# A selective-scan kernel: D·u added by the third scan, loads for the chained sums issued sooner, memsets issued later

## The chip, the cores and the metric

The kernel runs on one core of a Trainium2 chip. The metric is the device time of one execution in microseconds, as the median of several executions. All timed executions quoted below are in the fast state; one experiment was executed only once, and its state is unknown, which is said there. The ratios compare kernels that ran on the same chip in the same rounds.

Five engines matter: TensorE (PE, with its weight loads PEld), VectorE (DVE), ScalarE (ACT), GpSimd (POOL), and SyncE (SP), which here only issues transfers, all of them from one queue in program order.

## The reference

The reference is one vision block on a 4x64x64x96 image: group norm, a convolutional branch with a four-direction selective scan, then linear attention and a small quantized feed-forward network. The change touches the scan and what follows it.

```python
def selective_scan(u, delta, A, Bs, Cs, D, delta_bias):     # K = 4 directions, Dn = 192, N = 16, L = 4096
    delta = jax.nn.softplus(delta + delta_bias[None, :, :, None])
    def step(h, inp):
        ut, dt, Bt, Ct = inp
        dA = jnp.exp(dt[..., None] * A[None])
        h = dA * h + (dt * ut)[..., None] * Bt[:, :, None, :]
        y = jnp.einsum('bkdn,bkn->bkd', h, Ct)
        return (h, y)
    ...
    return y + D[None, :, :, None] * u
...
# the four directions: rows, columns, and both of them backwards
inv_y = jnp.flip(out_y[:, 2:4], axis=-1)
y = out_y[:, 0] + inv_y[:, 0] + wh_y + invwh_y
# layer norm of y, times silu(z), projection; x = x + that
# t = tokens of x
t = t + attention(norm(t))          # q (k^T v), six heads
t = t + ffn(norm(t))
```

D·u can be added in any one direction, with the four D summed, since u is the same array in another order. That is the freedom that the change uses.

## The kernel before

The scan is cut into 1536 pieces: 4 batches, 4 directions in the order `KORD` = 1, 3, 0, 2, 4 chunks of 1024 time steps, 6 groups `g` of 32 channels, and 4 quarters `q` of the state. A piece is a 128x1024 tile. I call the 96 pieces of one batch and direction a stage. One piece takes:

- (First, per group of four pieces, SyncE loads two tiles named dl: delta, and delta·u.)
- ACT: `dA = exp(anm·dl)` into PSUM, two buffers, emitted one piece ahead.
- GpSimd: `w = dl·B`, emitted four pieces ahead ("inject").
- DVE: the scan `h = dA·h + w`, in one instruction.
- The product `w = h·C`: on DVE (903 pieces) or on GpSimd (633), dealt by a tally of estimated costs.
- PE: sums the product over the state into `yp` in PSUM (one buffer), three pieces late. In the last quarter of a group it also adds what earlier directions left, which `load_sums` has fetched into the tile `ya`. These are the chained sums.
- ACT: copies `yp` to SBUF every eight pieces ("ys"), and SyncE stores it two pieces later.

```python
p = SimpleNamespace(w=pool("wp", 9), ..., ya=pool("yap", 1), ..., dl=pool("dlp", 3), ...)

def load_sums(self, i):
    b, e, ci, g, q = self.pieces[i]
    k = KORD[e]
    if k < 2:
        return
    at = CH * (NCH - 1 - ci)
    t = c.p.ya.tile([128, 3, 256], F32, name=f"ya_{i}", tag="ya")
    whole = lambda d: d.rearrange("h p l -> (h p) l")
    srcs = [c.yd[1][b]] if k == 3 else [c.yd[0][b], whole(c.y13[b]), whole(c.ud[b])]
    for j, src in enumerate(srcs):
        c.nc.sync.dma_start(t[:, j], src[32 * g : 32 * g + 32, at : at + CH].rearrange("d (x l) -> x d l", x=4))
    self.sums[i // NQ] = [(t[:, j, ::-1], c.dskip[:, g] if j == 2 else c.back4) for j in range(len(srcs))]

def reduce(self, i):
    ...                                   # y: the PSUM tile, prod: the product w
    more = self.sums.pop(i // NQ, []) if q == NQ - 1 else []
    for x in range(4):
        c.nc.tensor.matmul(y[32 * x : 32 * x + 32, g % 2, :], c.sum4, prod[:, 256 * x : 256 * x + 256], ...)
    for n, (src, w) in enumerate(more):
        c.nc.tensor.matmul(y[:, g % 2, :], w, src, start=False, stop=(n == len(more) - 1))

# the scan's loop, one turn per piece
for i in range(n):
    self.loads(i)                 # at q == 3: dl of the group three ahead, 2 x 512 KB; B and C now and then
    if i % NQ == NQ - 1:
        ...                       # (waits in program order until the turned y is made)
        self.load_sums(i)
    if i >= 1:
        self.carry(i - 1)         # ACT
    if i % 8 == 3 and i > 8:
        self.evacuate(i - 4)      # ACT: ys
    if i + 1 < n:
        self.decay(i + 1)         # ACT: dA
    if i >= 3:
        self.reduce(i - 3)        # PE
    if i + AHEAD < n:
        self.inject(i + AHEAD)    # GpSimd
    self.late_product()           # GpSimd
    self.scan(i)                  # DVE
    c.later.tick()                # SyncE: stores that are due
    ...                           # one step each of: the next deltas, the other work ("back")
```

Beside the scans, one step per piece, run the next batches' prologue and the epilogue of the batch that is done. Two pieces of it are touched besides the memsets:

```python
c.vec.tensor_tensor(m0, self.vks, c.hmask, ALU.mult)      # middle(): 96x96, once per batch

while nxt:                                                # last(): attention and its residual, per 512 tokens
    q, tt = nxt
    x1 = ln.load("x1b", f"x1b{q}", [96, 512])
    nc.sync.dma_start(x1, c.x1d[b][:, cols])
    ...
    c.vec.tensor_tensor(x2, ps, x1, ALU.add)
```

Of the kernel before, what the change touches and what calls it, by code (L numbers as in the profile page):

```python
# [11 lines left out]
F32 = mybir.dt.float32  # L12
# [4 lines left out]
ALU = mybir.AluOpType  # L17
# [4 lines left out]
NB, IH, IW, DM = 4, 64, 64, 96  # L22
# [3 lines left out]
CH = 1024  # L26
NCH = L // CH
HID = 384
NQ8 = L // 512
NG, NQ = DN // 32, NS // 4  # L30
# [23 lines left out]
def hybrid_kernel(ctx: ExitStack, tc: tile.TileContext, a: dict, out: bass.AP):  # L54
    nc = tc.nc
# [3 lines left out]
    def pool(name, bufs, **kw):  # L59
        return ctx.enter_context(tc.tile_pool(name=name, bufs=bufs, **kw))  # L60

    const, dram = pool("const", 1), pool("dram", 1, space=DRAM)
    p = SimpleNamespace(
        w=pool("wp", 9), y=pool("yp", 2), cy=pool("cyp", 2), h=pool("hp", 2), ya=pool("yap", 1), pu=pool("pup", 1), pd=pool("pdp", 2),
        f=pool("fp", 8), bc=pool("bcp", 5), dl=pool("dlp", 3), dA=pool("dAp", 2, space=PSUM),
        ps=pool("psp", 1, space=PSUM),
    )
# [33 lines left out]
    c = SimpleNamespace(nc=nc, a=a)  # L101
# [55 lines left out]
    def weights():  # L157
# [200 lines left out]
        dg = temp("dg", [128, 3, 2])  # L358
        nc.vector.tensor_copy(dg, ps[:, 0:6].rearrange("p (g h) -> p g h", h=2))
        for g in range(NG):  # L360
            nc.vector.tensor_scalar(dskip[:, g], back4, dg[:, g % 3, g // 3 : g // 3 + 1], None, ALU.mult)
        nc.vector.memset(on192, 1.0 / DN)
        nc.vector.memset(on96, 1.0 / DM)
        nc.vector.tensor_scalar(mean96, i96, -1.0 / DM, None, ALU.add)
# [112 lines left out]
def prologue(c, b, xts=None):  # L477
# [11 lines left out]
    with tc.tile_pool(name=f"xg_{b}", bufs=1) as xgp:  # L489

        xg = xgp.tile([128, 2, L], F8, name=f"xg_{b}", tag="xg")
        xgw = xg.bitcast(F32)
        nc.gpsimd.memset(xgw[64:128, 1], 0.0)
        with tc.tile_pool(name=f"cv_{b}", bufs=1) as cvp:
            xsT = cvp.tile([DM, L], F8, name=f"xsT_{b}", tag="xsT")
            tflat = [cvp.tile([96, (IH + 2) * (IW + 2)], F8, name=f"tp{h}_{b}", tag=f"tp{h}") for h in range(2)]
# [40 lines left out]


            sub.close()
            for h in range(2):  # L540
                nc.gpsimd.memset(tflat[h].bitcast(F32), 0.0)
            for h in range(2):
# [96 lines left out]
        with tc.tile_pool(name=f"rw_{b}", bufs=1) as rw:  # L639
# [4 lines left out]
            tbg, sgg = (t.rearrange("p (g r) -> p g r", r=64) for t in (tbc, sgn))  # L644
            g2 = rw.tile([128, 2, 320], F8, name=f"g_{b}", tag="g")
            gw = g2.bitcast(F32)
            nc.gpsimd.memset(gw[:, :, 48:80], 0.0)
            for o in (1, 0):
                xr = rw.tile([128, 96, 64], BF16, name=f"xr{o}_{b}", tag="xr")
                xm = xr.rearrange("p (m i) g -> p i m g", m=3)  # L650
# [27 lines left out]
                for gh in range(2):  # L678
# [41 lines left out]
                        )  # L720
                    yield
                c.later.flush()
                for x, k in enumerate((o, o + 2)):
                    nc.sync.dma_start(gw[:, x, 0:48], c.sgd[b][k].rearrange("(p f) -> p f", p=128))
                    yield
                    yield
                    gp = bank(f"gp{k}", k // 2).rearrange("p (s f) -> p s f", s=4)
                    for s in range(4):
                        nc.tensor.matmul(
                            gp[:, s, :], g2[:, x, 48 * s : 48 * s + 128], c.ident8, start=True, stop=True  # L730
                        )
                    yield
                    t = rw.tile([48, 4, 32], F32, name=f"gt_{b}_{k}", tag="gt", bufs=2)
                    nc.scalar.activation(t.bitcast(F8), gp[0:48], AF.Copy, saturate=False)
                    nc.sync.dma_start(c.gTd[b][k], t)
# [30 lines left out]
class Epilogue:  # L766
# [9 lines left out]
    def open(self):  # L776
        c, p, b = self.c, self.c.p, self.b
        ep = self.ep = self.ctx.enter_context(c.tc.tile_pool(name=f"ep_{b}", bufs=1))
        self.vks = ep.tile([DM, DM], F32, name=f"vks_{b}", tag="vks")
        self.ms = [ep.tile([DM + (i == 2), DM], F32, name=f"m{i}_{b}", tag=f"m{i}") for i in range(3)]  # L780

        tts = [ep.tile([DM + 1, 512], F32, name=f"tt{i}_{b}", tag=f"tt{i}") for i in range(2)]
        for tt in tts:
            c.nc.gpsimd.memset(tt[DM : DM + 1, :], 1.0)
        self.lane = SimpleNamespace(
            f32=lambda nm: p.f.tile([128, 512], F32, name=f"{nm}_{b}", tag="f"),
            bank=lambda nm, j: p.ps.tile([128, 512], F32, name=f"{nm}_{b}", tag=f"b{j}"),
            load=lambda key, nm, shape, dt=F32: ep.tile(shape, dt, name=f"{nm}_{b}", tag=key),
            tts=tts, x={},
        )  # L790
        self.opened = True
# [63 lines left out]
        return r  # L855

    def sums(self, ln):
        nxt = None
        while nxt is not None or self.todo or not self.opened:
            q, nxt = nxt, None  # L860
            if q is None:
                q = self.take()
                if q is None:
                    yield
                    continue
                self.loads(ln, q, ("ys", "sz", "xb"))
                yield
                yield
            got = []
            yield from self.norm(ln, q, got)  # L870
            nxt = got[0]
# [117 lines left out]
    def middle(self):  # L989
        c, nc, ln, mm = self.c, self.c.nc, self.lane, self.mm  # L990
        c.later.flush()
        m0, m1, m2 = self.ms
        c.vec.tensor_tensor(m0, self.vks, c.hmask, ALU.mult)
        ps = ln.bank("m1", 1)[0:96, 0:96]
        mm(ps, [(m0, c.wff)])
        yield
        nc.scalar.copy(m1, ps)
        ps = ln.bank("m2", 0)[0 : DM + 1, 0:96]
        mm(ps, [(c.wqT, m1)])
        yield  # L1000
        c.vec.tensor_tensor(m2, ps, c.bff, ALU.add)

    def last(self, ln):
# [3 lines left out]
        def fetch(n):  # L1007
# [4 lines left out]
            nc.sync.dma_start(tt[0:96, :], c.td[b][:, 512 * q : 512 * q + 512])  # L1012
            return q, tt

        def bank(nm, j):
            return ln.bank(f"{nm}{q}", j)

        n = 0
        nxt = fetch(n)
        while nxt:  # L1020
            q, tt = nxt
            cols = slice(512 * q, 512 * q + 512)
            x1 = ln.load("x1b", f"x1b{q}", [96, 512])
            nc.sync.dma_start(x1, c.x1d[b][:, cols])
            n += 1
            nxt = fetch(n)

# [6 lines left out]
            yield  # L1034
            x2 = f32("x2")[0:96]
            c.vec.tensor_tensor(x2, ps, x1, ALU.add)
            pc = bank("fc", 1)[0:96]
            mm(pc, [(c.mean96, x2)])
            yield
# [49 lines left out]
class Scans:  # L1089
# [173 lines left out]
    def load_sums(self, i):  # L1263

        c = self.c
        b, e, ci, g, q = self.pieces[i]
        k = KORD[e]
        if k < 2:
            return
        at = CH * (NCH - 1 - ci)  # L1270
        t = c.p.ya.tile([128, 3, 256], F32, name=f"ya_{i}", tag="ya")
        whole = lambda d: d.rearrange("h p l -> (h p) l")
        srcs = [c.yd[1][b]] if k == 3 else [c.yd[0][b], whole(c.y13[b]), whole(c.ud[b])]
        for j, src in enumerate(srcs):
            c.nc.sync.dma_start(  # L1275
                t[:, j], src[32 * g : 32 * g + 32, at : at + CH].rearrange("d (x l) -> x d l", x=4)
            )
        self.sums[i // NQ] = [(t[:, j, ::-1], c.dskip[:, g] if j == 2 else c.back4) for j in range(len(srcs))]

    def reduce(self, i):  # L1280

# [28 lines left out]
    def run(self, back):  # L1310
        c, lanes, n = self.c, [], len(self.pieces)

        w = [c.p.w.tile([128, CH], F32, name=f"w_s{x}", tag="w") for x in range(7)]
        ps = [c.p.dA.tile([128, CH], F32, name=f"dA_s{x}", tag="dA") for x in range(2)]
        for x in range(3):
            half = slice(512 * (x % 2), 512 * (x % 2) + 512)
            lanes.append(
                self.prepare((
                    w[x].rearrange("p (t l) -> p t l", t=2), w[3 + x // 2][:, half], w[5 + x // 2], ps[x // 2][:, half],
                ))  # L1320
            )
        interleave(lanes)
        for q in range(NQ):
            self.load_bc(0, self.bt, 0, 0, 0, q)
            self.load_bc(1, self.ct, 0, 0, 0, q)
        while lanes:
            interleave(lanes)
            c.later.tick()
        c.later.flush()
        self.load_dl(0)  # L1330
        for m in (1, 2):
            self.load_dl(m)
        self.decay(0)
        for i in range(AHEAD):
            self.inject(i)
        for i in range(n):
            self.at = i
            self.loads(i)
            if i % NQ == NQ - 1:
                while KORD[self.pieces[i][1]] == 2 and self.pieces[i][0] not in c.turned:  # L1340
                    next(back)
                self.load_sums(i)
            if i >= 1:
                self.carry(i - 1)
            if i % 8 == 3 and i > 8:
                self.evacuate(i - 4)
            if i + 1 < n:
                self.decay(i + 1)
            if i >= 3:
                self.reduce(i - 3)  # L1350
            if i + AHEAD < n:
                self.inject(i + AHEAD)
            self.late_product()
            self.scan(i)
            c.later.tick()
            if i % 8 == 1 and self.todo:
                while (self.todo[0][0], self.todo[0][1] % 2) not in c.ready:
                    next(back)
                lanes.append(self.prepare())
            interleave(lanes)  # L1360
            next(back, None)
            if i > n - 64:
                next(back, None)
        self.late_product()
        for i in range(n - 3, n):
            self.reduce(i)
        self.evacuate(n - 1)
        c.later.flush()
        self.at = 2 * n
# [76 lines left out]
```

## Time and profile before

| | before |
|---|---|
| median of 3 runs | 5713.55 us (5709.6 to 5714.53) |
| span of the profiled run | 5710.5 us, mean granted TensorE clock 0.663 |
| DVE / POOL busy | 5157.6 / 5075.9 us |
| ACT / PE busy | 3566.1 / 3355.5 us |
| DVE idle by direction 1, 3, 0, 2 (over four batches) | 70, 46, 49, 138 us |

DVE and POOL are the full engines; the idle in the stages is what a change of waits can win. The last row comes from cutting the trace at every 96th decay and taking the length of each stretch less DVE's busy time; it is one profiled run and good to about 5 us a cell.

The prediction shows the page, the stretches and one hole. Here are lines that it only quotes or does not have, from the list of waits: who waited, for whom, then the total in us, how many times, and the longest.

```profile
POOL w L401 <- DVE h L401: 121.5, 106, 4.2
...
DVE x L401 <- DMA x1b<-x1d: 13.4, 4, 4.6
```

GpSimd waits 106 times for DVE's `h`, while DVE waits for a product of GpSimd in 31 us in all; and one load, `x1b`, stops DVE itself. The next list is that of SyncE's own queue.

```profile
SPq L1198 <- ACT dA L1221: 846.1, 216, 13.0
...
SPq L1275 <- PE yp L1294: 84.8, 44, 7.6
```

SyncE stands 216 times, 3.9 us on average, before a dl load until ACT has finished a decay: the dl tile of the group being scanned is the buffer that the load will refill. Everything behind it in the queue stands too. About half of it, 440 us in 110 times, falls into the stages of directions 3 and 2, which are the ones that load `ya` (the same view, cut at the stages' ends). I had seen only the second of these lines when I predicted, and the first also belong here more.

### The profile page before, as it was taken

The numbers are of one execution on the slowest core, as the hardware profiler recorded it, in microseconds if no ns is written. First come the engines' busy times: TensorE is split into PE (matmuls) and PEld (weight loads), VectorE is DVE, ScalarE is ACT, GpSimd is POOL, SyncE is SP. The second block draws the span as 40 slices with busy tenths as digits, with TensorE's granted clock in tenths as the row PEclk, the third lists the DMA queues.
The fourth block names the chain that finished last, engine by engine and source line by source line (L and its number), as shares of the span: only waits on it lengthen the run. The fifth ranks groups of instructions, "written<-read, shape, count | busy, mean of one in ns | idle before, by whom it ended". The sixth has DMA issues, their size and how long they took to land. (4 is left out here: it accounts for less than half of the span.)

```text
span 5710.5 us, 61945 instructions
## 1 busy us (share of the span) xinstructions
PE 3355.5 (59%) x19813; PEld 1348.7 (24%) x19813; DVE 5157.6 (90%) x3396; ACT 3566.1 (62%) x5564; POOL 5075.9 (89%) x2295
## 2 busy tenths in 40 slices
PE   6456754566557766566656765534776554334677
PEld 3222222222222222222222222111232111111233
DVE  3299999999899999999989999999999999999884
ACT  4467766776566667776666667755556665555544
POOL 2299999999899999999899999999999999999881
PEclk8666765577667765567667776655786665555777
DMA  4455666766666566656666556655665555655652
GB/s 78 120 191 184 202 194 190 231 199 194 188 207 189 192 197 194 217 198 209 194 195 202 190 187 196 225 185 188 205 216 186 175 186 192 208 172 185 206 166 62
DMA packets 613245, 1069.91 MB, mean 187 GB/s; under 512 B 225084, under 2 KB 343925, under 8 KB 611125
## 3 DMA queue, kind: packets, MB, share of 16 engines
q1 hardware_dynamic: 599428, 1065.88, 59.3%
q8 instruction: 156, 2.56, 0.2%
q10 hardware_dynamic: 13488, 0.07, 0.1%
q14 instruction: 173, 1.41, 0.1%
HBM read 833.20 MB, written 229.38 MB: 186 GB/s over the span
## 5 line engine op out<-in xcount | busy, mean ns | idle before, releaser
L401 POOL TENSOR_TENSOR w<-dl,bc 128x1024 f32<-128x1024 f32 x1536 | 3581.3, 2358 | 151.7 <-PE yp L1289 74.3
L1221 ACT ACTIVATE dA<-dl,anm 128x1024 f32<-128x1024 f32 x1536 | 1715.5, 1117 | 460.4 <-DVE w L401 271.8
L1289 PE MATMUL yp<-w,sum 128*32 128x256 f32 x12288 | 1363.2, 551 | 1009.6 <-POOL w L401 580.4
L401 DVE TENSOR_TENSOR_SCAN dA<-dA,cy,w 128x1024 f32<-128x1024 f32 x678 | 1587.8, 2342 | 108.9 <-ACT dA L1221 97.9
L401 POOL TENSOR_TENSOR w<-h,bc 128x1024 f32<-128x1024 f32 x633 | 1490.4, 2355 | 127.7 <-DVE h L401 121.5
L401 DVE TENSOR_TENSOR w<-dA,bc 128x1024 f32<-128x1024 f32 x903 | 1105.8, 1225 | 62.6 <-DMA bc<-bcd 4.7
L401 DVE TENSOR_TENSOR_SCAN h<-dA,cy,w 128x1024 f32<-128x1024 f32 x474 | 1108.0, 2339 | 30.5 <-ACT dA L1221 30.5
L1289 PEld LDWEIGHTS yp<-w,sum 128*32 128x32 f32 x12288 | 342.4, 136 | 2080.9 <-POOL w L401 882.2
L401 DVE TENSOR_TENSOR_SCAN dA<-dA,w 128x1024 f32<-128x1024 f32 x225 | 513.5, 2282 | 29.4 <-ACT dA L1221 24.8
L1261 ACT COPY cy<-dA 128x1 f32<-128x1 f32 x678 | 105.9, 156 | 671.6 <-DVE w L401 670.2
L1294 PE MATMUL yp<-ya,back 128*128 128x256 f32 x576 | 286.0, 607 | 253.9 <-DMA ya<-yd 222.7
L577 PE MATMUL cv<-tp,cw 96*96 96x512 fp8e5 x1152 | 385.3, 481 | 77.3 <-ACT r L627 68.5
L401 DVE TENSOR_TENSOR_SCAN h<-dA,w 128x1024 f32<-128x1024 f32 x159 | 362.0, 2278 | 25.6 <-POOL w L401 25.6
L1294 PEld LDWEIGHTS yp<-ya,back 128*128 128x128 f32 x576 | 131.0, 274 | 423.4 <-DMA ya<-yd 281.4
L577 PEld LDWEIGHTS <-cw 96*96 96x96 fp8e5 x1152 | 161.7, 151 | 283.1 <-issue 237.0
L1261 ACT COPY cy<-h 128x1 f32<-128x1 f32 x474 | 88.2, 186 | 198.9 <-DVE h L401 198.4
L1303 ACT COPY ys<-yp 128x512 f32<-128x512 f32 x192 | 112.2, 585 | 122.9 <-PE yp L1294 112.7
L1164 ACT ACTIVATE pd<-dps,dbias,pvd 128x512 f32<-128x512 f32 x189 | 144.0, 762 | 27.9 <-PE dps L1159 27.8
L1165 ACT ACTIVATE sp<-dps,dbias,pvd 128x512 f32<-128x512 f32 x189 | 144.7, 766 | 0.0
L848 PE MATMUL yc<-eys,mean 96*96 96x512 f32 x240 | 130.5, 695 | 21.7 <-DMA esz<-szd 7.6
L401 DVE TENSOR_TENSOR pd<-dps,pu 128x512 f32<-128x512 f32 x189 | 130.6, 691 | 7.0 <-DMA pu<-ud 0.6
L401 DVE TENSOR_TENSOR dps<-dps,sp 128x512 f32<-128x512 f32 x189 | 129.1, 683 | 0.0
(280 smaller groups left out, 4059.6 us busy)
## 6 DMA issues: line engine op xcount, KB each, us to landing
dl<-dld SPq DMA_DIRECT2D x768, 512.0 KB
bc<-bcd SPq DMA_DIRECT2D x512, 512.0 KB
dld<-pd SPq DMA_DIRECT2D x126, 512.0 KB
yd<-ys SPq DMA_DIRECT2D x768, 64.0 KB
dld<-pd SPq DMA_DIRECT2D x126, 256.0 KB
ya<-yd SPq DMA_DIRECT2D x192, 128.0 KB
pu<-ud SPq DMA_DIRECT2D x32, 512.0 KB
pu<-utd SPq DMA_DIRECT2D x31, 512.0 KB
```

The source lines that it names most:

```text
L401: return getattr(self.eng, name)(out, *args, **kw)
L577: nc.tensor.matmul(ps, c.cw[:, j, t, 96 * h : 96 * h + 96], tpad[j][:, 8 * q + dy : 8 * q + dy + 8, dx : dx + IW], start=(j == 0 and t == ...
L848: self.c.nc.tensor.matmul(ps, w, x, start=(i == 0), stop=(i == len(pairs) - 1))
L1164: nc.scalar.activation(d[:, 0], ps, AF.Abs, scale=sc, bias=bi)
L1165: nc.scalar.activation(t, ps, AF.Relu, scale=sc, bias=bi)
L1221: c.nc.scalar.activation(t, self.dlt[i // NQ][0], AF.Exp, scale=c.anm[:, g, NQ * KORD[e] + q : NQ * KORD[e] + q + 1])
L1261: self.c.nc.scalar.copy(self.carries[g, q], h[:, CH - 1 : CH])
L1289: c.nc.tensor.matmul(y[32 * x : 32 * x + 32, g % 2, :], c.sum4, prod[:, 256 * x : 256 * x + 256], start=(q == 0), stop=(q == NQ - 1 and no ...
L1294: c.nc.tensor.matmul(y[:, g % 2, :], w, src, start=False, stop=(n == len(more) - 1))
L1303: c.nc.scalar.copy(t, y[:, :, ::-1] if k >= 2 else y)
```

## The change

Its intent: spare the last stage, the only one with three loads per group, one of them, by adding D·u in the third stage, where nothing was added; make room by that for a second `ya` buffer (a tile shrinks from three slots to two); issue the loads two steps sooner; take single waits off DVE (x1) and GpSimd (memsets that came first in a fresh pool and waited for its space). The parts hang together. When I built them separately, two `ya` buffers of three slots did not fit into SBUF (23.6 kB asked for, 22.6 left), and the sooner load with a single buffer deadlocked in the build, since it would have to precede the matmuls that free the buffer. One line is not in the change's name: a 96x96 product, `m0`, moves from DVE to GpSimd.

```diff
-        w=pool("wp", 9), ..., ya=pool("yap", 1), ...
+        w=pool("wp", 9), ..., ya=pool("yap", 2), ...
-            nc.vector.tensor_scalar(dskip[:, g], back4, dg[...], None, ALU.mult)
+            nc.vector.tensor_scalar(dskip[:, g], ident, dg[...], None, ALU.mult)
     # load_sums
-        if k < 2:
+        if k == 1:
             return
-        at = CH * (NCH - 1 - ci)
-        t = c.p.ya.tile([128, 3, 256], F32, name=f"ya_{i}", tag="ya")
+        at = CH * (NCH - 1 - ci if k >= 2 else ci)
+        t = c.p.ya.tile([128, 2, 256], F32, name=f"ya_{i}", tag="ya")
-        srcs = [c.yd[1][b]] if k == 3 else [c.yd[0][b], whole(c.y13[b]), whole(c.ud[b])]
+        srcs = {3: [c.yd[1][b]], 0: [whole(c.ud[b])], 2: [c.yd[0][b], whole(c.y13[b])]}[k]
...
     # the scan's loop
-            if i % NQ == NQ - 1:
+            if i % NQ == 1:
                 while KORD[self.pieces[i][1]] == 2 and self.pieces[i][0] not in c.turned:
                     next(back)
                 self.load_sums(i)
     # three memsets: xg after the first part of a prologue, g after the first turn, tt after the first loads
-        nc.gpsimd.memset(xgw[64:128, 1], 0.0)
...
+            nc.gpsimd.memset(xgw[64:128, 1], 0.0)
-            nc.gpsimd.memset(gw[:, :, 48:80], 0.0)
...
+                if o:
+                    nc.gpsimd.memset(gw[:, :, 48:80], 0.0)
-        for tt in tts:
-            c.nc.gpsimd.memset(tt[DM : DM + 1, :], 1.0)
...
+                if not self.begun and ln is self.lane:
+                    for tt in ln.tts:
+                        c.nc.gpsimd.memset(tt[DM : DM + 1, :], 1.0)
     # middle
-        c.vec.tensor_tensor(m0, self.vks, c.hmask, ALU.mult)
+        c.gps.tensor_tensor(m0, self.vks, c.hmask, ALU.mult)
     # last: x1 of the next turn is loaded right after the addition that frees the tile
+        x1 = residual(nxt[0]) if nxt else None
         while nxt:
-            x1 = ln.load("x1b", f"x1b{q}", [96, 512])
-            nc.sync.dma_start(x1, c.x1d[b][:, cols])
...
             c.vec.tensor_tensor(x2, ps, x1, ALU.add)
+            if nxt:
+                x1 = residual(nxt[0])
```

More of the change, by code (lines that the diff above doesn't have):

```diff
@@ L63, in hybrid_kernel @@
     p = SimpleNamespace(
-        w=pool("wp", 9), y=pool("yp", 2), cy=pool("cyp", 2), h=pool("hp", 2), ya=pool("yap", 1), pu=pool("pup", 1), pd=pool("pdp", 2),
+        w=pool("wp", 9), y=pool("yp", 2), cy=pool("cyp", 2), h=pool("hp", 2), ya=pool("yap", 2), pu=pool("pup", 1), pd=pool("pdp", 2),
         f=pool("fp", 8), bc=pool("bcp", 5), dl=pool("dlp", 3), dA=pool("dAp", 2, space=PSUM),
@@ L360, in weights @@
         for g in range(NG):
-            nc.vector.tensor_scalar(dskip[:, g], back4, dg[:, g % 3, g // 3 : g // 3 + 1], None, ALU.mult)
+            nc.vector.tensor_scalar(dskip[:, g], ident, dg[:, g % 3, g // 3 : g // 3 + 1], None, ALU.mult)
         nc.vector.memset(on192, 1.0 / DN)
@@ L857, in sums @@
     def sums(self, ln):
-        nxt = None
+        c, nxt = self.c, None
         while nxt is not None or self.todo or not self.opened:
@@ L1013, in fetch, with residual @@
             return q, tt
+        def residual(q):
+            x1 = ln.load("x1b", f"x1b{q}", [96, 512])
+            nc.sync.dma_start(x1, c.x1d[b][:, 512 * q : 512 * q + 512])
+            return x1
         def bank(nm, j):
@@ L1277, in load_sums @@
             )
-        self.sums[i // NQ] = [(t[:, j, ::-1], c.dskip[:, g] if j == 2 else c.back4) for j in range(len(srcs))]
+        if k == 0:
+            self.sums[i // NQ] = [(t[:, 0], c.dskip[:, g])]
+        else:
+            self.sums[i // NQ] = [(t[:, j, ::-1], c.back4) for j in range(len(srcs))]
     def reduce(self, i):
```

## The prediction

> **What bounds the kernel now.** I read the page's busy shares first, then the busy time of each engine in each of the sixteen scan stages, then the lists of waits, then the timeline of the worst hole. The page says which engines are full:
>
> ```profile
> PE 3355.5 (59%) x19813; PEld 1348.7 (24%) x19813; DVE 5157.6 (90%) x3396; ACT 3566.1 (62%) x5564; POOL 5075.9 (89%) x2295
> ```
>
> VectorE (DVE) and GpSimd (POOL) share the scan work almost evenly; a static tally in the program deals the products out between them. Everything else is at about 60%. The busy strips show that the two are at 90% or more from slice 3 to slice 38, so the missing 10% is mostly the start (196 us idle on DVE in the first 285 us) and the end (74 us in the last 143). In between there are about 280 us of idle on each. To see where, I cut the trace where the decay activations pass each multiple of 96 (the stages run in the order direction 1, 3, 0, 2 for each of four batches). The third and fourth stage of the first batch and of the second, from the busy time by stretch (columns: PE, PEld, DVE, ACT, POOL busy, clock, DMA):
>
> ```profile
> 923.00:1249.00 326.00, 183.07 (x1197) 70.89 (x1198) 310.89 (x193) 235.75 (x358) 310.11 (x137) 0.60 0.66 208
> 1249.00:1608.00 359.00, 219.45 (x1381) 95.22 (x1380) 321.20 (x209) 229.10 (x357) 321.47 (x141) 0.72 0.66 198
> ...
> 2269.00:2596.00 327.00, 199.78 (x1170) 75.45 (x1170) 314.25 (x196) 240.90 (x369) 315.75 (x139) 0.60 0.65 206
> 2596.00:2947.00 351.00, 230.76 (x1388) 100.01 (x1387) 319.09 (x208) 228.58 (x357) 319.61 (x140) 0.68 0.65 202
> ```
>
> Length minus DVE busy is the idle: 15 and 13 us in the third stages, 38 and 32 in the fourth. Over all four batches the stages of direction 1, 3, 0, 2 leave DVE 70, 46, 49 and 138 us idle. The fourth stage is the one that loads three arrays for the sum (another direction's y, the turned y, and u for D·u). The waits, from the list over the whole run:
>
> ```profile
> PE yp L1289 <- POOL w L401: 580.4, 188, 10.4
> ...
> PEld yp L1294 <- DMA ya<-yd: 281.4, 85, 10.3
> PE yp L1294 <- DMA ya<-yd: 222.7, 78, 9.8
> ...
> DVE dA L401 <- ACT dA L1221: 122.8, 70, 10.0
> ...
> ACT ys L1303 <- PE yp L1294: 112.7, 44, 10.6
> ...
> POOL w L401 <- PE yp L1289: 74.3, 43, 6.3
> ```
>
> TensorE idles, which alone would cost nothing. But the evacuation "ACT ys" waits for it, the next decay "ACT dA" stands behind that copy, and the DVE scan waits for the decay. One such hole in the timeline, first batch, fourth stage:
>
> ```profile
> 1405.22 0.57 SPq L1275 DMA_DIRECT2D ya<-yd  x1
> ...
> 1406.44 0.55 SPq L1275 DMA_DIRECT2D ya<-ud  x1
> ...
> 1412.97 1.22 PE L1294 MATMUL yp<-ya,back 128*128 128x256 f32 x2 [4.99 <-DMA ya<-yd]
> 1415.39 1.22 PE L1294 MATMUL yp<-ya,back 128*128 128x256 f32 x2 [1.20 <-DMA ya<-y]
> 1417.30 1.22 PE L1294 MATMUL yp<-ya,dskip 128*128 128x256 f32 x2 [0.69 <-DMA ya<-ud]
> 1418.56 0.58 ACT L1303 COPY ys<-yp 128x512 f32<-128x512 f32 x1 [6.87 <-PE yp L1294]
> 1419.04 1.12 ACT L1221 ACTIVATE dA<-dl,anm 128x1024 f32<-128x1024 f32 x1
> ```
>
> The three loads land 7.8, 9.6 and 10.9 us after issue, about 2 us apart, behind two dl loads of 512 KB issued just before them. They are issued three steps ahead of their matmul, and a step is about 3.5 us (326 us / 96), so 10.4 us minus what SyncE is late. They are just too late; the next DVE scan starts at 1420.20 after 5.99 us of idle.
>
> **What the Trainium skill says.** "TensorE: Matmul & The Clock Gate", "Architectural detail", calls ScalarE's and VectorE's queues strict FIFO: so a copy that waits holds back the decay behind it, as this trace shows (6.87 us on ACT, 5.99 on DVE). "PSUM — Partial Sum Buffer", "Engine vs sequencer instructions", says matmuls start and complete in program order: a matmul waiting for ya therefore also holds other products' sums, and with them the w buffers GpSimd wants (74.3 us above). [...] here the wait is 8 to 11 us, so queueing[...] dominates. "Perfetto Trace Analysis", "Optimization Strategy", reads a gap repeating on the engine that should be full as a possible lack of buffers; ya has one buffer, and SyncE's queue waited 84.8 us (44 times) for its matmuls to release it.
>
> **The change, part by part.**
> 1. D·u moves from the last stage to the third, as a plain (not reversed) load. Counts stay: 96 u loads of 128 KB and 96 extra matmul pairs move. The last stage has two loads per group instead of three, the third one instead of none.
> 2. The ya loads are issued two steps (7 us) sooner, into two buffers instead of one, and now ahead of that group's dl loads rather than behind them. Lead is five steps, 17.5 us, against a landing of at most 11. So I take nearly all ya waits as gone. Worth: I matched every DVE gap of 1.5 us or more with an ACT gap just before it that ended with "PE yp L1294". They are 4.3 in direction 3; 3.1, 2.8, 6.0, 3.4, then 2.3, 3.6, 2.3, 2.7, then 5.6, 1.9, 1.5, then 3.3 in the four last stages; 4.4, 3.2, 2.9 just after stage ends: sum 53 us. Indirect ones, where PE was late with the epilogue's matmuls behind ya (2.9 and 4.3 us in the last stage), and gaps under 1.5 us I estimate at 10 to 15 together. About **65 us**.
> 3. x1 for the attention residual is loaded an iteration ahead: "DVE x <- DMA x1b" is 13.4 us, directly on DVE. All of it: **13 us**.
> 4. Memsets later. Each waited for the tile pool's space: xg 11.0 and 8.6, g 10.7, 7.5 and 11.1, tt 3.8, 7.4, 7.7 and 10.6 us, 78 us of GpSimd idle inside the scans. But DVE rarely waits for GpSimd (31 us in all, 26 of it at the start), while GpSimd waits 121.5 us for DVE's h: GpSimd usually runs ahead and absorbs the stall. Also ACT's "xr" copy waits for the same store as the g memset and stays. I count **5 us**.
> 5. One 96x96 product per batch goes to GpSimd: DVE saves 4 x 0.25 us, GpSimd may wait a few us for vks, and in the drained tail it costs a fraction of a us. **0**, or -2.
> 6. The tail: the last evacuation waited 10.6 us, of which ya explains only the end (5594 to 5598). **2 us**.
>
> Sum 85 us at most; some of what is removed will be found again as DVE waiting for GpSimd, since both are equally loaded (5157 and 5076 us) and each hole also lets the other catch up. I take off 7 and predict **5635 us**, 1.4% less.
>
> **Rivals.**
> A: *ya waits were hidden anyway.* TensorE's idle before ya (281.4 us at weight loads and 222.7 at matmuls, much of it the same stretches) suggests much, but stages of direction 3, which also wait on ya (24.5 us in the first), have only 7 to 15 us DVE idle. If DVE's holes come from the epilogue and prologue work that also falls into the fourth stage (gT and tbc waits of 10.0, 7.6, 3.3 and 4.3 us are there and stay), only 30 to 40 us come back: 5675.
> B: *Everything counts.* If the GpSimd stalls are as costly as the DVE ones, because both have no slack over a stage (their idle per stage is nearly equal, 38 and 37 us in the worst), the fourth stages fall to the idle of the others (138 to about 60), and 78 us of memset stalls give another 30 to 40: 5590.
> C: *The cost moves to the third stage or to SyncE.* The third stage gets a load and a wait per group; SyncE issues ya before dl, so dl lands later. The dl loads are three groups ahead (some 40 us) and the DMA share is 0.66 at most, so I expect under 10 us.
> D: *GpSimd becomes the bound* when DVE's holes close. Its own stalls (74 behind yp, 78 memsets) fall too, so it should keep pace.
>
> **Range and chances.** A to B spans 5675 to 5590, with 5635 between. I take 5598 to 5672 for 8 in 10. Faster by over 2% means below 5599: 0.1. Slower by 2% has no mechanism: 0.01. Within 2%: 0.89.
>
> **What would show it.** Right: the wait "ACT ys <- PE yp L1294" falls from 112.7 to under 25; "PE yp L1294 <- DMA ya" nearly disappears; "DVE dA <- ACT dA" falls from 122.8 to about 65; fourth stages of about 335 us or less; "DVE x <- DMA x1b" gone; memset waits on GpSimd gone, its wait for DVE's h about as large as before or larger. Wrong: if ya waits vanish and fourth stages stay at 350, rival A holds; if DVE's wait for w, or waits for dl, grow by tens of us, C or D; if the idle falls in stages without ya loads, the memsets were worth more than I gave them.

## The result, and the profile after

The changed kernel takes 5609.33 us (median of 4 runs, 5604.07 to 5612.69), the kernel before 5711.87 us in the same rounds (median of 4). The ratio of the fast runs is 0.9819, with a 95% interval of 0.9802 to 0.9836. Ratios here and below are the mean time of one kernel's fast runs over that of the other's of the same rounds, so not quite the ratio of the medians quoted. The gain of 1.8% is some 103 us. It falls within 2% as predicted and inside the range (5598 to 5672), 26 us better than the number itself (5635).

The busy times from the page of the changed kernel:

```profile
PE 3325.3 (59%) x19813; PEld 1340.1 (24%) x19813; DVE 5136.9 (92%) x3392; ACT 3564.0 (64%) x5564; POOL 5079.3 (91%) x2299
```

DVE lost 20.7 us of work and GpSimd gained 3.4. The rest of the gain is idle time. The same third and fourth stages of the first and second batch (columns: PE, PEld, DVE, ACT, POOL busy, clock, DMA):

```profile
916.00:1244.00 328.00, 201.80 (x1243) 81.84 (x1244) 312.42 (x193) 236.05 (x359) 312.30 (x138) 0.64 0.69 218
1244.00:1578.00 334.00, 200.17 (x1357) 87.87 (x1357) 319.91 (x209) 228.87 (x357) 320.46 (x140) 0.73 0.67 204
2224.00:2549.00 325.00, 204.25 (x1216) 81.47 (x1216) 313.97 (x196) 240.52 (x369) 315.64 (x140) 0.65 0.69 218
2549.00:2883.00 334.00, 204.44 (x1364) 89.26 (x1364) 319.60 (x208) 229.01 (x358) 320.63 (x140) 0.71 0.66 205
```

The fourth stages went from 359 and 351 us to 334 each, while the work of DVE in them changed by 1.3 and 0.5 us. The third stages, which got the u loads, hardly changed in length (326 and 327 us before, 328 and 325 after). Over all batches the DVE idle by direction is now 60, 36, 47 and 79 us. The sum falls from 303 to 222, that is 81 us, and with the 21 us of work it makes 102 of the 103 measured (the two profiled runs differ by 106). So the start and the end, outside the stages, have no large part in it.

The waits after, in the same columns:

```profile
PE yp L1300 <- POOL w L401: 478.2, 177, 9.1
...
POOL w L401 <- DVE h L401: 101.8, 117, 4.4
...
DVE dA L401 <- ACT dA L1229: 85.7, 66, 5.6
...
POOL w L401 <- PE yp L1300: 63.6, 39, 5.7
...
ACT ys L1314 <- PE yp L1305: 25.3, 14, 8.0
...
DVE h L401 <- ACT dA L1229: 11.8, 10, 3.6
...
PE yp L1305 <- DMA ya<-ud: 1.9, 1, 1.9
```

The evacuation's wait for the added matmuls fell from 112.7 to 25.3 us, and what those matmuls waited for loads from 222.7 us for `yd` alone to 1.9. DVE's waits for a decay fell from 122.8 and 30.5 to 85.7 and 11.8. `x1b` is out of DVE's list, and of the memsets' nine waits inside the scans (78 us) none is left; a tenth, of 8.3 us in the start, was there before and stays. PE's waits for products fell by a hundred us and its waits for the evacuation rose from 382 to 595, which costs or gains nothing by itself. And the `m0` product, before and after, as the view of its tile shows it (minimum, median and maximum in ns of the four):

```profile
L401 DVE TENSOR_TENSOR m<-vks,hmask x4: 253/5581/7134, 1996.8 to 5633.1; 96x96 f32<-96x96 f32 x4
```

```profile
L401 POOL TENSOR_TENSOR m<-vks,hmask x4: 382/387/439, 1963.1 to 5523.6; 96x96 f32<-96x96 f32 x4
```

On DVE it had taken up to 7.1 us, although the shortest took 0.25. I had not read this row when I predicted, and it was the first surprise.

### The profile page after: what moved, and what is told of

Same layout as the page of the kernel before. It is cut to its first block, busy times and chain, and to the rows that moved or that the text cites. A ratio compares the mean times of both kernels' runs of the same rounds, so it can differ in the third digit from the quotient of the medians.

```text
span 5604.2 us, 62024 instructions
## 1 busy us (share of the span) xinstructions
PE 3325.3 (59%) x19813; PEld 1340.1 (24%) x19813; DVE 5136.9 (92%) x3392; ACT 3564.0 (64%) x5564; POOL 5079.3 (91%) x2299
## 5 line engine op out<-in xcount | busy, mean ns | idle before, releaser
L401 POOL TENSOR_TENSOR w<-h,bc 128x1024 f32<-128x1024 f32 x633 | 1489.8, 2354 | 117.1 <-DVE h L401 101.8
L1305 PE MATMUL yp<-ya,back 128*128 128x256 f32 x576 | 250.3, 558 | 0.0
L1167 PE MATMUL dps<-gT,wdz 128*128 128x64 fp8e5 x1008 | 113.3, 309 | 35.1 <-DMA gT<-gTd 35.1
L1314 ACT COPY ys<-yp 128x512 f32<-128x512 f32 x192 | 112.2, 584 | 30.0 <-PE yp L1305 25.3
```

Source lines behind the costliest of these rows:

```text
L401: return getattr(self.eng, name)(out, *args, **kw)
L1167: nc.tensor.matmul(pv[:, s], wd[:, k, s], gT[:, :, c0 : c0 + 16], start=True, stop=True)
L1314: c.nc.scalar.copy(t, y[:, :, ::-1] if k >= 2 else y)
```

## The experiments

Twelve kernels ran, all with correct results. Except for one, each was timed in five rounds beside the kernel before; the intervals are about 0.0014 to either side, or 8 us. The first eight take the change apart, in both directions: single parts added to the kernel before, and single parts taken out of the changed one.

| kernel | what it is | median us | ratio to before | 95% |
|---|---|---|---|---|
| ya_u | before + sooner `ya` loads, two buffers, u in the third stage | 5655.02 | 0.9901 | 0.9888 to 0.9915 |
| u_only | before + u in the third stage | 5690.15 | 0.9965 | 0.9951 to 0.9978 |
| memsets_only | before + later memsets | 5686.99 | 0.9963 | 0.9950 to 0.9975 |
| x1_only | before + x1 an iteration ahead | 5697.99 | 0.9975 | 0.9961 to 0.9989 |
| m0_only | before + `m0` on GpSimd | 5708.46 | 0.9999 | 0.9985 to 1.0014 |
| late_two_buf | after, `ya` loads at the old step | 5644.82 | 0.9879 | 0.9865 to 0.9892 |
| no_mem | after, memsets at their old place | 5633.15 | 0.9859 | 0.9845 to 0.9872 |
| no_m0 | after, `m0` back on DVE | 5616.02 | 0.9831 | 0.9818 to 0.9845 |
| late_ahead | after, `ya` at the old step but issued before dl | 5603.29 | 0.9809 | 0.9795 to 0.9822 |
| swap_only | before + `ya` issued before dl | 5675.99 | 0.9921 | 0.9907 to 0.9935 |
| gt_early | after + the next batch's sign tile loaded sooner | 5590.06 | 0.9784 | 0.9771 to 0.9798 |
| two_sbuf | after + 32 small DVE products of two SBUF tiles | 5705.1 (1 run) | | |

The kernel before had medians of 5712.13 us beside the first batch of these (ya_u, memsets_only, x1_only, m0_only), 5712.33 beside the second (u_only, late_two_buf, no_mem, no_m0), 5711.86 beside the third (late_ahead, gt_early, two_sbuf) and 5717.33 beside swap_only.

### Chained sums and D·u together: ya_u

```diff
+ ya pool 1 -> 2 buffers of two slots; dskip from ident; load_sums with u for k == 0
-            if i % NQ == NQ - 1:
+            if i % NQ == 1:
```

> The kernel before with the ya part alone: two steps of lead, two buffers, D u moved to the third scan. Theory Y (prediction: ScalarE's evacuation behind late ya loads makes VectorE's holes): 55 to 70 us gained, the fourth stages shrink by 15 to 25 us each, ScalarE's evacuation wait falls from 112.7 to about 25 us. Rival A: 30 to 40 us.

0.9901, some 57 us. The evacuation's wait for the added matmuls, "ACT ys" for "PE yp" in the list of waits, falls from 112.7 us (44 times) to 34.1 (20). DVE's two waits for a decay fall from 153.3 us together to 102.3, so most of the 57 us arrives by the way PE, ACT, DVE. DVE's idle falls from 138 to 91 us in the fourth stages, and rises from 49 to 57 in the third, where the u loads are now. So the part that I took for the largest is that, and close to the 65 us that I gave it; the new cost in the third stage is about 8 us.

### D·u alone: u_only

```diff
+ ya tile of two slots, still one buffer; dskip from ident; load_sums with u for k == 0
             if i % NQ == NQ - 1:        # unchanged
```

> The kernel before with only D u moved to the third scan: two ya slots, one buffer, loads still three steps ahead. The ya part alone gave 57 us. Theory Y1 (lead is what counts: three steps are too few for any load behind two dl loads): under 20 us gained, because the first ya load still lands 7 to 8 us after issue; the third landing, some 2 us later, is all that goes. Theory Y2 (the third load is what is too late): 30 to 50 us.

0.9965, some 20 us. The evacuation's wait is 92.1 us (49 times): one load of three fewer leaves most of the waits in place. DVE's idle in the fourth stages falls by 37 us (138 to 101), but in the third, where the u load now stands behind dl, it rises by 21 (49 to 70). The second buffer and the sooner load are worth the other 37 us of ya_u.

### The sooner load alone taken back: late_two_buf

```diff
-            if i % NQ == 1:
+            if i % NQ == NQ - 1:
```

> The changed kernel with the ya loads issued three steps ahead again, still two buffers and D u in the third scan. Theory Y1: the time rises by 35 to 50 us over the changed kernel (ratio to before about 0.990), ScalarE's wait behind ya comes back to 60 us or more. Theory Y2: within 15 us of the changed kernel (ratio about 0.984).

0.9879 against 0.9819: 34 us of the changed kernel's gain go with this one line. Its waits:

```profile
PE yp L1305 <- DMA ya<-yd: 218.2, 74, 8.9
...
ACT ys L1314 <- PE yp L1305: 77.4, 41, 8.9
```

So the second buffer and the lighter fourth stage leave these 34 us on the table; when the load is issued decides about them. But "when" has two sides: two steps, some 7 us, and the place in SyncE's queue, since at the old step the dl loads of the same step stand ahead. The timeline of one group of the fourth stage, first batch (start, duration, engine):

```profile
1376.50 6.16 SPq L1206 DMA_DIRECT2D dl<-dld  x2
...
1382.75 0.56 SPq L1283 DMA_DIRECT2D ya<-yd  x1
...
1390.24 1.20 PE L1305 MATMUL yp<-ya,back 128*128 128x256 f32 x2 [2.96 <-DMA ya<-yd]
...
1391.88 1.22 PE L1305 MATMUL yp<-ya,back 128*128 128x256 f32 x2 [0.45 <-DMA ya<-y]
```

### The place in the queue: late_ahead

To tell them apart I kept the old step and only put `ya` ahead of dl in it.

```diff
-            self.loads(i)
-            if i % NQ == 1:
+            if i % NQ == NQ - 1:
                 ...
                 self.load_sums(i)
+            self.loads(i)
```

> The three-step variant of the changed kernel (ratio 0.9879) with one swap: in the same step the ya loads are issued ahead of the group's two dl loads instead of behind them. Theory P (place in SyncE's queue: there the ya loads stood behind dl issues that waited for a free buffer, and behind 1 MB of data): most of the 34 us between 0.9879 and 0.9819 comes back, ratio 0.982 to 0.984, ScalarE's wait behind ya falls from 77 to under 45 us. Theory T (the two steps themselves): ratio 0.986 to 0.989, wait above 60 us.

0.9809: at the old step, and as fast as the changed kernel (0.9819; the intervals overlap). The same group:

```profile
1369.46 5.65 SPq L1283 DMA_DIRECT2D ya<-yd  x1
...
1375.80 1.20 SPq L1206 DMA_DIRECT2D dl<-dld  x2
...
1381.58 1.13 PE L1305 MATMUL yp<-ya,back 128*128 128x256 f32 x4
```

In both kernels the first issue of this step takes about 6 us, whichever load it is (it follows the same store, `utd<-ut`, and the trace does not say what it spends them on). With dl first, `ya` is issued at 1382.75, and its matmul can start 7.5 us later, having waited 2.96 us for it. With `ya` first, the matmul waits for nothing and dl bears the delay, which has three groups of time. Over the whole run:

```profile
PE yp L1305 <- DMA ya<-ud: 46.5, 18, 6.4
...
ACT ys L1314 <- PE yp L1305: 25.2, 13, 9.2
```

PE still waits for `ya`, 46.5 us for the `ud` loads of the third stage and 11.2 for the `yd` loads, more than in the changed kernel, but these reach the evacuation no more than there (25.2 against 25.3 us). So the two steps are not needed. It is enough that `ya` does not stand behind dl.

Standing behind dl can cost time before the issue of `ya` (SyncE is held) and after it (1 MB of dl goes first). The packed traces tell when each load landed. Counted from the last decay of its group, the mean of the 192 `yd` loads is issued 4.6 us sooner in late_ahead than in late_two_buf, and lands 6.0 us after its issue instead of 7.2. In swap_only, below, it is issued 2.4 us sooner than in the kernel before and lands 5.2 us after its issue instead of 6.7. So both count, and the time before the issue counts more. No run here separates the two.

### The place in the queue alone: swap_only

```diff
-            self.loads(i)
             if i % NQ == NQ - 1:
                 ...
                 self.load_sums(i)
+            self.loads(i)
```

> The kernel before with one swap and nothing else: in each fourth step the ya loads (still up to three, one buffer, three steps ahead, D u in the last scan) are issued ahead of the group's two dl loads. Theory P (the place behind the dl loads made ya late): most of the 57 us of the whole ya part, ratio 0.989 to 0.992, ScalarE's wait behind ya from 112.7 to under 50 us. Theory P2 (place alone is not enough with one buffer, whose release the queue must await, and three loads in a row): 15 to 35 us, ratio 0.994 to 0.997, wait above 60 us.

0.9921, some 45 us, from moving one line of the kernel before, with three loads per group and one buffer. The evacuation's wait falls from 112.7 to 46.4 us. SyncE's own waits show what goes on, and what is left:

```profile
SPq L1198 <- ACT dA L1221: 485.6, 154, 13.0
...
SPq L1275 <- PE yp L1294: 304.4, 88, 11.5
```

Before, the first of these was 846.1 us and the second 84.8. The whole fall of the first lies in directions 3 and 2 (from 440 us to 79); in the other two, without `ya`, it stays at 406. With `ya` first, the queue no longer makes `ya` wait for a decay of ACT; instead it makes both wait, 304.4 us in all, for the matmuls that release the only `ya` buffer. The second buffer removes that, and u's move makes its room. So for the chained sums the wait in the queue comes first and the buffer second. The three effects are not additive: swap_only gives 45 us, u_only 20, ya_u with both and the second buffer 57.

### The memsets: memsets_only and no_mem

```diff
 memsets_only: the three memset hunks of the change, on the kernel before
 no_mem:       the same three hunks reversed, on the changed kernel
```

> The kernel before with only the three kinds of GpSimd memsets moved later. Theory S (GpSimd runs ahead and absorbs those stalls; the prediction's 5 us): 2 to 10 us gained, GpSimd's wait for VectorE's h grows. Rival B (both engines have no slack): 30 to 40 us gained, and the idle of VectorE in stages without ya loads falls by about 10 us in each stage that had a memset stall.

> The changed kernel with the memsets back in their early places. If their worth of 21 us alone is additive: ratio about 0.9855. If it overlaps with what the ya part frees: ratio about 0.983 (under 8 us).

Alone they give 0.9963, some 21 us; taken out of the changed kernel they cost 0.9859 against 0.9819, some 23 us. I had given them 5. In memsets_only GpSimd then waits more for others, so it did get ahead: 138.7 us for DVE's `h` and 104.9 for PE to release products, against 121.5 and 74.3 before. In no_mem the waits that differ from those of the changed kernel are on DVE for ScalarE, not for GpSimd:

```profile
DVE dA L401 <- ACT dA L1227: 99.5, 74, 7.3
...
DVE h L401 <- ACT dA L1227: 16.8, 13, 7.2
```

116.3 us together against 97.5 after, 19 us more; and GpSimd waits only 69.8 us for DVE's `h`, against 101.8 after. DVE's direct wait for GpSimd is the same, 25.9 us in two places at the start. The timeline of one stall in no_mem shows the way from the memset to DVE:

```profile
3671.48 0.98 POOL L784 MEMSET tt<- 1x512 f32 x2 [8.94 <-DMA y<-yh]
...
3677.24 1.08 PE L1298 MATMUL yp<-w,sum 128*32 128x256 f32 x8 [13.85 <-POOL w L401]
...
3679.51 0.59 ACT L1312 COPY ys<-yp 128x512 f32<-128x512 f32 x1 [6.00 <-PE yp L1303]
...
3681.22 2.36 DVE L401 TENSOR_TENSOR_SCAN dA<-dA,cy,w 128x1024 f32<-128x1024 f32 x1 [4.66 <-ACT dA L1227]
```

GpSimd stood 8.94 us before the memset of `tt`, waiting for the space of another tile that a transfer still used. Its products came late; PE waited 13.85 us for one; the evacuation on ACT waited 6.00 us for PE; the decay behind it in ACT's order came late; and DVE waited 4.66 us, listed under "ACT dA". So this stall of GpSimd cost DVE about half of itself, through two other engines, and a list of DVE's direct waits for GpSimd does not show it. In memsets_only, too, the gain stands there: DVE's two waits for a decay are 135.8 us together against 153.3 before. Over the run it is 21 to 23 us for some 78 us of stalls removed.

Which of the three memsets carries the gain I did not run separately. The `g` memset seems to be worth nothing: at its place DVE's gap was 3.23, 1.82 and 2.84 us in the first three batches before, and 3.20, 1.93 and 1.83 after, since ACT waits there for the same store; what that stall does later, through PE, these gaps do not show.

### The x1 load: x1_only

```diff
+        x1 = residual(nxt[0]) if nxt else None        # and after the addition: if nxt: x1 = residual(nxt[0])
-            x1 = ln.load("x1b", f"x1b{q}", [96, 512])
-            nc.sync.dma_start(x1, c.x1d[b][:, cols])
```

> The kernel before with only the residual's load moved one iteration ahead. If the 13.4 us that VectorE waited for it count in full: 10 to 14 us gained and that wait gone. If they are absorbed elsewhere: under 4 us, wait gone all the same.

0.9975, some 14 us for a wait of 13.4 us on DVE. A wait of the full engine itself came back whole here, as far as an interval of 8 us to either side can tell.

### The small product: m0_only, no_m0 and two_sbuf

```diff
 m0_only, on the kernel before (no_m0 is the reverse, on the changed one)
-        c.vec.tensor_tensor(m0, self.vks, c.hmask, ALU.mult)
+        c.gps.tensor_tensor(m0, self.vks, c.hmask, ALU.mult)
```

> The kernel before with one edit: the 96x96 product of vks and the head mask goes to GpSimd. Theory L (the VectorE form waits for GpSimd[...]: its three bodies inside the scans took 7.13, 6.04 and 5.12 us against 0.25 us when GpSimd was idle): VectorE's busy time falls by some 18 us and the time by 12 to 20 us. Rival (the prediction's item 5: nothing to gain): the time stays within 3 us of before.

> The changed kernel with the 96x96 product back on VectorE. Parts alone gave 57, 21, 14 and 1 us, 93 of the 103 measured. Theory L2 (VectorE's 18 us at that product counted only once its other holes were closed): ratio to before 0.9845 to 0.9855, some 15 us slower than the changed kernel. Rival (still absorbed): within 5 us of the changed kernel, ratio about 0.982.

m0_only removes 19.8 us of DVE's busy time (5157.6 to 5137.8), and gains nothing: 0.9999. DVE's waits for decays took its place: 138.2 us before the scans into `dA` and 32.3 before those into `h`, where they were 122.8 and 30.5, so 17 us more. Taken out of the changed kernel the same line costs 7 us (0.9831 against 0.9819), with overlapping intervals. Its worth is thus between nothing and some 10 us, and is not settled. What can be looked into is why the product took so long on DVE. The timeline of the kernel before, at the first of the four:

```profile
1996.76 7.13 DVE L401 TENSOR_TENSOR m<-vks,hmask 96x96 f32<-96x96 f32 x1
...
1996.84 2.35 POOL L401 TENSOR_TENSOR w<-h,bc 128x1024 f32<-128x1024 f32 x1
...
1999.14 4.63 POOL L401 TENSOR_TENSOR w<-dl,bc 128x1024 f32<-128x1024 f32 x2
```

When it starts, GpSimd is still in an earlier product (until 1996.87), and it ends 0.1 us after the third of the products that follow (2003.77). The Trainium skill has this in "SBUF — State Buffer", section "Who interferes with whom": a DVE instruction with two SBUF inputs contends with a GpSimd instruction that reads SBUF, while one with at most one SBUF input does not, outside the modes that use two ports. The traces agree: the 903 products of the scan, with one operand in PSUM, take 1.225 us each beside the same GpSimd work. To see whether it is the two SBUF operands and not this place in the program, I added 32 such products, of a tile that nobody else was writing, over the whole scan:

```diff
             self.scan(i)
+            if i % 48 == 20:
+                nc.vector.tensor_tensor(c.wff, c.wff, c.wff, ALU.max)     # leaves wff as it is
```

> The changed kernel with 32 more 96x96 elementwise products on VectorE, one every 48 pieces, both operands in SBUF, value unchanged (maximum of a tile with itself). Theory L (such an instruction waits for GpSimd's hold, as vks times mask did): mean 4 to 7 us each, at most a few of them near 0.25 us, VectorE busy up by 130 to 220 us, time up by 60 us or more. Rival (the 5 to 7 us were something special to that place): 0.25 us each, busy up 8 us, time up under 10 us.

```profile
L1367 DVE TENSOR_TENSOR wff<-wff x32: 228/2400/11685, 337.1 to 5485.7; 96x96 f32<-96x96 f32 x32
```

From 0.23 to 11.7 us for the same 96x96 instruction (five of the 32 took 0.34 or less), 111.9 us in all, 3.5 each. The one run took 5705.1 us, 96 more than the changed kernel's median (a single run, of unknown state). The expectation was somewhat too high in size, and right in kind. There is no run with 32 products of one SBUF operand at the same places; the 903 products above stand in for it. Here each of the 32 costs time at about its length, while the 18 us of `m0` did not. That DVE would have waited for ACT at those three places anyway fits the 17 us above, but is not shown.

### A wait that was left: gt_early

The list of waits after the change has one more load that is issued late: the matmuls for the deltas ("PE dps") wait three times for a sign tile ("DMA gT"), 35.1 us in all, the longest 15.0. The first direction of each later batch loads its sign tile only when its first delta is prepared. The same pattern as `ya`: issue it earlier, into the second of two buffers that is free.

```diff
+        if (ci, part) == (NCH - 1, 0) and k == KORD[-1] and (b + 1, KORD[0]) in c.ready:
+            self.load_signs(b + 1, KORD[0])
```

> The changed kernel with one more edit: the sign tile of the next batch's first direction is loaded at the last direction's last chunk instead of right before its first use. VectorE still has holes of 5.2, 2.0, 4.9 and 5.6 us there (TensorE waits 35 us for that load, three times). If these close: 8 to 18 us faster than the changed kernel, ratio to before 0.979 to 0.9805. If another wait takes the place (the tile's writer is just done anyway): within 5 us, ratio 0.981 to 0.983.

5590.06 us, 0.9784 (0.9771 to 0.9798): 19 us less than the changed kernel and faster than both kernels. The wait for `gT` is gone, ACT's wait for the deltas ("ACT pd" for "PE dps") falls from 21.0 to 10.0 us, and DVE's for decays from 85.7 to 73.9.

## Why the prediction was right or wrong

1. **What bounds the kernel, and the chain PE, ACT, DVE.** Right. Where the evacuation waits less for the added matmuls, DVE waits less for decays: ya_u alone took them from 153.3 to 102.3 us. After the whole change they are 85.7 and 11.8 us, and fourth stages of 334, 334, 330 and 350 us. The number I had given for the decays, 65, was too low by 21; the last fourth stage, with 35 us of DVE idle, keeps waits that the change does not touch.

2. **D·u and the `ya` loads, steps 1 and 2, 65 us.** Right in sign and size: 57 measured. The reason was misread in part. I put the worth into "two steps sooner" and named the queue only in passing, "and now ahead of that group's dl loads rather than behind them". late_ahead has the old step and the new order and is as fast as the change (0.9809). swap_only shows 45 us for the order alone, on the kernel before. What held `ya` up was its place behind dl: dl issues waited for a buffer (440 us of SyncE's time in the two directions with `ya`), and the load also landed more slowly after its own issue. Of the 3.8 us by which swap_only brings in the mean `yd` load sooner, 2.4 are before the issue and 1.4 after it. The prediction's own hole shows the second part: there `ya` lands 7.8 us after its issue.

3. **x1, 13 us.** Right: 14 measured.

4. **The memsets, 5 us. This is the step that failed**: 21 us measured alone, 23 when taken out. The sentence was "But DVE rarely waits for GpSimd (31 us in all, 26 of it at the start) ... GpSimd usually runs ahead and absorbs the stall." It read only the direct wait. The stall reaches DVE through PE and ACT, as the timeline of no_mem shows, and is booked there as a wait for a decay. Rival B had a part of it, "78 us of memset stalls give another 30 to 40", which was too much; the measured share is between the two. Two of the prediction's signs fit less well than the gain. GpSimd's wait for `h`, which was to stay or grow, grew with the memsets alone (138.7 us), but fell to 101.8 with the whole change, since ya_u alone takes it to 86.0. And the idle of direction 1, which has no `ya` loads, fell from 70 to 60 us, which was to be a sign of the memsets; but ya_u alone has the same 60 and memsets_only none of it (69).

5. **`m0`, 0.** The time was about right, 1 to 7 us and unsettled; the working was wrong. "DVE saves 4 x 0.25 us" took the length from the tail; in the three batches inside the scans it took 7.13, 6.04 and 5.12 us.

6. **The tail, 2 us, and the 7 us taken off.** The last evacuation waits 8.0 us instead of 10.6, but from the last decay to the end the two profiled runs have 124 and 125 us, so no gain shows there. The 7 us were not needed: DVE's direct waits for GpSimd went from 31 to 28 us, not up. The parts alone sum to 57 + 21 + 14 + 1 = 93 us, and the whole is 103. The difference is near what the intervals allow. The sum of my terms was 85 before the 7 were taken off; had the memsets been put at 21, it would have been 101. That the number came within 26 us is in part luck: 8 us too many for `ya` stand against 16 too few for the memsets.

7. **Rivals.** A is refuted by ya_u. B is nearest: its fourth stages were to fall to 60 us of idle and fell to 79, and it gave the memsets 30 to 40 us instead of 21; it came to 5590. C is right in its small form: 8 us in the third stages (21 in u_only, where u is loaded at the old place). D did not happen: POOL's busy share is 91%, and its waits for `h` fell only by 20 us.

What stays open: which memset carries how much; what `m0` is worth; how much of the place in the queue is the held issue and how much the data ahead; and what the first issue after the `utd` store spends 6 us on. A fourth dl buffer, or an issue of `ya` from another engine's queue, was not tried.

## What to carry to other kernels

In a queue that issues in order, put a load with a near deadline ahead of one that may have to wait for its buffer; looking at who waits in the issuing queue, and for what, was worth as much here as two steps of lead. When an engine that looks as if it had slack stalls, follow the stall through the engines that it feeds before calling it free: the full engine may list it under another name. And look at the longest, not only at the mean or at the shortest, of an instruction's durations.

## What the Trainium skill lacked or had wrong

- "SBUF — State Buffer", "SBUF: two separate sides", says whoever starts first has the shared pair of ports for the whole instruction and the other blocks. It gives no rule for a DVE instruction that meets back-to-back GpSimd instructions. In the kernel before, the DVE product started while one GpSimd product ran, 0.08 us before the next three, and ended after the last of them: 7.13 us for one that takes 0.25 alone, with GpSimd's at 2.35 each. In two_sbuf the longest was 11.7 us. Why it does not get its turn between them no run here shows.
- "DMA: Bandwidth & Descriptors", "Anatomy of one DMA", explains, for transfers issued from GpSimd, the time of one DMA from its issue on, about 2 us fixed; of a wait before it, it says only that the issuing sequencer does it. More of what the new place saved lay before the issue (2.4 us for the mean `yd` load of swap_only) than after it (1.4): dl loads waiting for their buffer held SyncE's queue for 846 us in 216 waits (440 us of it in the directions with `ya`), and putting `ya` ahead gave 45 us. I found no page that says how to order loads in one issuing queue.
- "Perfetto Trace Analysis", "Optimization Strategy", reads a repeating gap on the full engine as a possible lack of buffers. It does not mention the order of issue, which here was worth more than the `ya` buffer: 45 us for the order with one buffer (swap_only), against an estimate of 13 for the second buffer in the old order (late_two_buf's 69 us less 20, 21, 14 and 1 for the parts u, memsets, x1 and `m0` measured alone). The dl loads in front did wait for a buffer, so the reading holds for dl; more dl buffers were not tried.
